# Local attention: rotary products and squares taken from PSUM, halves swapped by a negative step, and mask and minimum of two heads in two instructions

## The chip, the cores and the metric

The kernel runs on one core of one Trainium2 chip. The metric is the device time of one execution of the whole program, in microseconds. Three runs of the kernel before took 2280.73, 2284.91 and 2290.02 us; the median is 2284.91 us.

## The reference, cut to what matters

The program is a sequence of eight stages over four batches of 512 positions with 128 channels: four attention blocks (causal, relative with rotary shift, ALiBi, Shaw's relative positions) and, between them, four other blocks. The second stage, called F0 in the kernel, is the one that the change rewrites. It is a small transformer of two layers with local attention, 8 heads of 64, window 64:

```
q, k = l2norm(q) * qs, l2norm(k) * ksc
q, k = q*cos*scale + rotate_half(q)*sin*scale, k*cos/scale + rotate_half(k)*sin/scale
sim  = einsum(q * 8, k of this window and of the one before)
sim  = where((i < j) | (i > j + 64) | (j == -1), -max, sim)
out  = softmax(sim) @ v
x = x + out @ wo;  h = layernorm(shift(x));  x = x + (a * gelu(g)) @ w2
```

Here rotate_half(x) is the pair (-x2, x1) of the two halves of a head's 64 values. The causal and the ALiBi stage (class Causal and its subclass Alibi), and the rotary stage (class Rel), subtract each row's maximum before the exponential; they compute these maxima with one instruction that adds a mask to a block of scores, writes the sum to a scratch tile that nobody reads, and gives the maximum along the row.

## The kernel before, in words

All stages share the five engines (in the profile PE is TensorE, with PEld for its weight loads, DVE VectorE, ACT ScalarE, POOL GpSimd, and SP the queue that issues most transfers). Python generators, one for each strand of work (projections of the next batch, scores of this one, the block behind the attention), are stepped in turn, and a tile framework with priorities then sets the final order of the instructions of each engine. Each engine works its instructions off in that order; waits between engines, and between instructions of one engine that reuse a buffer, are semaphores. A tile of a pool with a tag and bufs=n has n buffers in turn: the instruction that writes buffer n+1 waits until the users of buffer 1 are done.

F0 treats 8 units u (4 batches, 2 layers). For each unit, qkv (from L1525) transposes the input (L208), makes for every 128 rows c three products of three matmuls each (q, k, v; L298 to L300) in a PSUM bank "b" (three banks, which the block behind the attention uses too). For q and k, ScalarE copies the bank to SBUF (L1563: the tile ta for q, kr for k), squares it (L1566, tile sq, one buffer), VectorE multiplies the two halves of each head, swapped, by a table of sines into the tile tb (L1570, two instructions of 256 elements), then the tile itself by the cosines (L1572), and sums the squares of each head (L1573). For k, GpSimd adds the two products (L1586); for q, TensorE adds them when it transposes them into a bank "t". The reciprocal norms rn come from a chain of small VectorE instructions (L327 to L336, L1589, L1591), and k is scaled by them (L1597).

scores (from L1607) computes the scores of two heads in 16 matmuls (L1620) into two banks "s". score (from L1624), called for each head, runs four times, for blocks of 128 by 128: one VectorE instruction that adds the band mask, writes the sum to sm (one buffer) and gives the row's minimum times rn into nb (L1633; the page shows it as CUSTOM_DVE_ANT_0, followed by DVE_READ_ACCUMULATOR2_ANT, which stores the minimum), and one exponential on ScalarE with nb as bias and -1 as scale (L1635; its row sum is stored by ACTIVATION_READ_ACCUMULATOR) into p (four buffers of 512). Two heads later, turn transposes p (L208), ScalarE copies it to PT (L1645), and values multiplies by v (L1664). post (from L1674) is the block behind: division (L1697), output projection (L1703), the shifted tile h whose first row is cleared by GpSimd (L1707), yb = X + b2 on GpSimd (L1712), layernorm, the gated network (L1737, L1740, L1747, L1754) and the sum (L1757, L1760).

In the other attention stages the scratch tile of the maxima is called junk: L644 (Causal and Alibi, 256 instructions each, 128 to 512 elements) and L922 (Rel, 256 of 640 elements). It has two buffers. Stage A3 has a scratch tile of the same kind, jk (L1303), with one buffer; its scores sit in L1279 to L1285.

Of the kernel before, what the change touches and what calls it, by code (L numbers as in the profile page):

```python
# [16 lines left out]
P = 128  # L17
# [565 lines left out]
class Causal(Attn):  # L583
# [49 lines left out]
    def maxima(self, t, gs):  # L633
        k, nc, pool = self.k, self.nc, self.wk
        Ks = self.Ks[t % self.nb]
        mx = pool.tile([P, 4, 4], F32, tag="mx", name=f"mx{t}", bufs=2)
        for i in range(4):
            for qc in range(4):
                n = P * (qc + 1)
                nm = max(n, 256)  # L640
                s = k.bank("s")
                nc.tensor.matmul(s[:, :nm], self.qof(0, t, i)[:, qc * P:(qc + 1) * P], Ks[:, i, :nm], start=True, stop=True)  # L642
                junk = pool.tile([P, 512], BF16, tag="junk", name=f"junk{t}{i}{qc}", bufs=2)
                nc.vector.tensor_tensor_reduce(junk[:, :n], s[:, :n], k.mask[:, 512 - n:512], 1.0, NEG,  # L644
                                               ALU.add, ALU.max, mx[:, qc, i:i + 1])
                if i == 3 and qc == 3:
                    gs.append(self.rows_out(t, mx))
                yield
# [117 lines left out]
class Rel(Attn):  # L766
# [139 lines left out]
    def maxima(self, t, gs):  # L906
# [4 lines left out]
        for i in range(4):  # L911
            for qc in range(4):
# [8 lines left out]
                junk = pool.tile([P, 640], BF16, tag="junk", name=f"junk{t}{i}{qc}", bufs=2)  # L921
# [496 lines left out]
def f0_constants():  # L1418
# [17 lines left out]
    band = np.stack([band, band], 1)  # L1436
# [4 lines left out]
class F0:  # L1441
# [3 lines left out]
    wait_rn, wait_h, wait_h7, wait_ta, na, nbt, nta, la, np, ns, npt, pk = 6, 2, 8, 2, 4, 4, 2, 2, 4, 1, 3, 0  # L1445
    banks = dict(s=2, t=2, o=1, b=3)
# [5 lines left out]
    def setup(self):  # L1452
        k, nc, d, pool = self.k, self.k.nc, self.k.d, self.early
        self.band = k.load(pool, d["c_band"], [P, 2, P], "band", BF16, eng=nc.gpsimd)
        yield from self.weights_qkv(0)
        yield from self.weights_post(0)
# [68 lines left out]
    def qkv(self, u, X, tag="t"):  # L1525
# [25 lines left out]
        for c in range(4):  # L1551
            cs = slice(c * P, (c + 1) * P)
            for s in range(3):
# [4 lines left out]
                if s == 2:  # L1558
                    nc.scalar.copy(v[:, c, :], ps)
                    yield  # L1560
                    continue
                x = kr[:, c, :] if s else pool.tile([P, 512], F32, tag="ta", name=f"ta{u}{c}", bufs=self.nta)
                nc.scalar.copy(x, ps)  # L1563
                yield
                sq = pool.tile([P, 512], F32, tag="sq", name=f"sq{u}{c}{s}", bufs=1)
                nc.scalar.activation(sq, x, AF.Square)  # L1566
                tb = pool.tile([P, 8, 64], F32, tag="tb", name=f"tb{u}{c}{s}", bufs=2)
                x3 = x.rearrange("p (h d) -> p h d", d=64)
                for a, b2 in ((0, 32), (32, 0)):
                    nc.vector.tensor_tensor(tb[:, :, a:a + 32], x3[:, :, b2:b2 + 32],  # L1570
                                            w["tab"][:, 2 * s + 1, c, None, a:a + 32].to_broadcast([P, 8, 32]), ALU.mult)
                nc.vector.tensor_tensor(x3, x3, w["tab"][:, 2 * s, c, None, :].to_broadcast([P, 8, 64]), ALU.mult)  # L1572
# [17 lines left out]
        rn = pool.tile([P, 2, 4, 8], F32, tag="rn", name=f"rn{u}", bufs=2)  # L1590
        nc.vector.tensor_copy(rn.rearrange("p s c h -> p (s c h)"), k.rsqrt(pool, sf, 64, 1))  # L1591
# [15 lines left out]
    def scores(self, u, pr):  # L1607


        k, nc = self.k, self.nc  # L1610
        qT, kT = self.S[u][:2]
        if pr == 0:
            self.den[u] = self.early.tile([P, 4, 8], F32, tag="den", name=f"den{u}", bufs=2)
        self.s = [k.bank("s") for _ in range(2)]
        with k.front():
            for w in range(8):
                c, o = w // 2, 64 * (w % 2)
                for e in range(2):
                    r = slice(64 * e, 64 * e + 64)
                    m = nc.tensor.matmul(self.s[e][o:o + 64, c * P:c * P + P], qT[r, pr, 64 * w:64 * w + 64], kT[r, pr, 64 * w:64 * w + P], start=True, stop=True)  # L1620
                    if w == e == 0 and self.emptied:
                        k.waits(m.ins, self.emptied)

    def score(self, u, h):  # L1624

        k, nc, pool = self.k, self.nc, self.pool
        rn, den, s = self.S[u][3], self.den[u], self.s[h % 2]
        p = self.p[8 * u + h] = pool.tile([P, 4, P], F32, tag="p", name=f"p{u}{h}", bufs=self.np)
        nb = pool.tile([P, 4], F32, tag="nb", name=f"nb{u}{h}", bufs=3)
        sm = pool.tile([P, 4, P], F32, tag="sm", name=f"sm{u}{h}", bufs=self.ns)  # L1630
        for c in range(4):

            m = nc.vector.tensor_tensor_reduce(sm[:, c, :], s[:, c * P:c * P + P], self.band[:, min(c, 1), :],  # L1633
                                           rn[:, 0, c, h:h + 1], 3.0e38, ALU.add, ALU.min, nb[:, c:c + 1])
            nc.scalar.activation(p[:, c, :], sm[:, c, :], AF.Exp, bias=nb[:, c:c + 1], scale=-1.0, accum_out=den[:, c, h:h + 1])  # L1635
        self.emptied = m.ins

    def turn(self, u, h):
        k, nc, pool = self.k, self.nc, self.pool
        p = self.p.pop(8 * u + h)  # L1640
# [33 lines left out]
    def post(self, u, X):  # L1674
# [32 lines left out]
        nc.gpsimd.memset(h[0:1, 0, 64:], 0.0)  # L1707
# [3 lines left out]
        yb = k.sh.tile([P, 4, P], F32, tag="r", name=f"yb{u}", bufs=1)  # L1711
        nc.gpsimd.tensor_tensor(yb, Y, w["b2"][:, None, :].to_broadcast([P, 4, P]), ALU.add)  # L1712
# [15 lines left out]
        nc.vector.tensor_tensor(xl, t, xh.bitcast(F32), ALU.subtract)  # L1728
        yield
# [51 lines left out]
    def run(self, Xs):  # L1781
# [9 lines left out]
        self.p, self.emptied = {}, None  # L1791
# [533 lines left out]
```

## Time and profile before

| | us |
|---|---|
| median of three runs | 2284.91 |
| the profiled execution | 2285.95 |
| its span | 2284.3 |
| TensorE busy (matmuls) | 2025.2 (89%) |
| VectorE busy | 1682.8 (74%) |
| ScalarE busy | 1334.6 (58%) |
| GpSimd busy | 581.1 (25%) |
| mean granted TensorE clock | 0.958 of full |

Busy time is the time in which an engine has at least one instruction running; instructions of one engine overlap a little, so that the distance from start to start of two that follow each other is shorter than their duration. By the first and last starts of their lines, the maxima of Causal (L644) run from 27.6 to 231.7 us, F0's scores from 249.0 to 654.2 us, Rel's maxima from 681.5 to 1063.3 us, and Alibi's from 1173.7 to 1425.6 us; neighbouring stages overlap at their ends, and the projections of F0's first unit run from 157.9 us on.

### The profile page before, as it was taken

To read this page: it belongs to the slowest core of one execution; us is meant where nothing else is said; L and a number is where in the kernel's file an instruction comes from. 1 tells how busy PE (TensorE), PEld (TensorE's weight loads), DVE (VectorE), ACT (ScalarE), POOL (GpSimd) and SP (SyncE) were. 2 spreads that over 40 slices of the span, in tenths; PEclk is the share of its full clock that TensorE was granted. 3 is DMA by queue.
4 is the path that set the end of the run, shared out by engine and by line. 5 is a ranking of instruction groups with operands and counts; after the bars stand their busy time and mean duration, and the time that the engine had idled before them with its cause. 6 is when DMAs were issued, how large, how long until landed. Compare 5 with 4: busy or idle time off the path is not lost.

```text
span 2284.3 us, 42095 instructions
## 1 busy us (share of the span) xinstructions
PE 2025.2 (89%) x13888; PEld 1467.8 (64%) x13888; DVE 1682.8 (74%) x5589; ACT 1334.6 (58%) x2982; POOL 581.1 (25%) x775
## 2 busy tenths in 40 slices
PE   6989787888778889898999999899899999999897
PEld 4665566666656556665788666677666666665676
DVE  5778688688878777775677877552778878778787
ACT  3656786677753456566332666332777777777632
POOL 2222212111212655555200222522111111111221
PEclk9999998899997989999999999999899999999999
DMA  6221311111341543521220330412889888788400
GB/s 185 91 75 34 98 50 44 24 28 30 109 132 33 177 144 95 154 79 34 69 65 1 116 105 30 153 68 57 202 212 213 207 195 191 187 215 202 117 5 15
DMA packets 265507, 242.31 MB, mean 106 GB/s; under 512 B 106368, under 2 KB 190634, under 8 KB 264522
## 3 DMA queue, kind: packets, MB, share of 16 engines
q1 hardware_dynamic: 260058, 222.12, 36.1%
q0 software_dynamic: 5232, 17.50, 3.3%
q8 instruction: 111, 1.82, 0.3%
q14 instruction: 106, 0.87, 0.1%
HBM read 103.03 MB, written 74.32 MB: 78 GB/s over the span
## 4 chain that ended last, share of the span: by engine, by line
PE 48%; DVE 12%; ACT 8%; POOL 5%; DMA 5%; issue 4%; SPq 1%; ACTq 0%; POOLq 0%; DVEq 0%
PE t L208 4%; PE s L2047 4%; PE o L1328 3%; PE o L967 3%; PE o L1946 3%; PE b L298 2%; PE s L298 2%; PE s L300 2%; PE s L299 2%; POOL Pt L1012 2%; PE o L691 2%; PE s L1279 2%; PE s L1280 2%; PE b L299 2%; PE b L300 1%
## 5 line engine op out<-in xcount | busy, mean ns | idle before, releaser
L922 DVE CUSTOM_DVE_ANT_0 junk<-w,a1mask 128x640 bf16<-128x640 f32 x256 | 204.4, 818 | 77.5 <-PE w L920 75.8
L208 PE MATMUL t<-ident,p 128*128 128x128 f32 x1280 | 203.5, 280 | 19.6 <-ACT p L1285 13.8
L718 ACT ACTIVATE Pt<-t 128x384 f32<-128x384 f32 (+1 forms) x384 | 178.2, 536 | 52.6 <-PE t L675 41.0
L208 PEld LDWEIGHTS t<-ident,p 128*128 128x128 f32 x1280 | 151.7, 142 | 80.0 <-ACT p L1285 35.7
L1298 ACT COPY PT<-t 128x512 f32<-128x512 f32 x256 | 150.2, 596 | 77.7 <-PE t L208 76.8
L993 ACT ACTIVATE Pt<-t 128x512 f32<-128x512 f32 x256 | 150.0, 599 | 71.9 <-PE t L992 49.1
L1285 ACT ACTIVATE p<-s,nb 128x512 f32<-128x512 f32 x256 | 178.8, 703 | 13.9 <-DVE nb L1284 7.6
L1284 DVE TENSOR_REDUCE nb<-s 128x1 f32<-128x512 f32 x256 | 175.0, 687 | 2.5
L644 DVE CUSTOM_DVE_ANT_0 junk<-s,a0mask 128x128 bf16<-128x128 f32 (+3 forms) x256 | 114.3, 486 | 41.5 <-PE s L642 40.9
L1303 DVE CUSTOM_DVE_ANT_0 jk<-p,a3right 128x496 bf16<-128x496 f32 (+3 forms) x256 | 124.1, 485 | 26.0 <-ACT p L1285 14.6
L644 DVE CUSTOM_DVE_ANT_0 junk<-s,a2mask 128x128 bf16<-128x128 f32 (+3 forms) x256 | 115.7, 485 | 28.2 <-PE s L642 27.4
L727 POOL TENSOR_SCALAR_AFFINE_SELECT Pt<-Pt 128x512 f32<-128x512 f32 x112 | 71.8, 653 | 228.7 <-ACT Pt L718 211.9
L1282 DVE TENSOR_TENSOR s<-s,W 128x160 f32<-128x160 f32 (+1 forms) x256 | 81.3, 319 | 65.5 <-PE s L1280 64.3
L1279 PE MATMUL s<-a3KT,a3QT 128*128 128x512 f32 x256 | 119.0, 467 | 7.7 <-DMA a3KT<-H 2.4
L1635 ACT ACTIVATE p<-sm,nb 128x128 f32<-128x128 f32 x256 | 101.3, 399 | 30.5 <-DVE nb L1633 29.9
L1328 PE MATMUL o<-PT,V 128*64 128x512 f32 x512 | 116.9, 599 | 0.5 <-ACT PT L1298 0.5
L1280 PE MATMUL s<-a3K,a3Q 128*128 128x512 f32 x256 | 102.7, 402 | 0.0
L1633 DVE CUSTOM_DVE_ANT_0 sm<-s,band,rn 128x128 f32<-128x128 f32 x256 | 78.4, 345 | 30.3 <-PE s L1620 22.4
L990 PE MATMUL t<-a1Q,a1K 128*128 128x512 f32 (+3 forms) x256 | 93.0, 370 | 6.1 <-ACT Pt L993 1.9
L967 PE MATMUL o<-Pt,a1va 128*32 128x128 f32 (+3 forms) x896 | 69.5, 453 | 26.9 <-POOL Pt L1012 26.8
L1933 ACT ACTIVATE sl<-s 128x512 f32<-128x512 f32 x64 | 38.1, 600 | 90.4 <-PE s L300 75.9
L1321 POOL CAST a<-at 128x256 fp32r<-128x256 f32 x32 | 13.0, 406 | 304.8 <-DMA at<-a3dpw 162.1
(497 smaller groups left out, 5983.9 us busy)
## 6 DMA issues: line engine op xcount, KB each, us to landing
W<-a3dsk SPq DMA_DIRECT2D x32, 640.0 KB
a1Q<-a1iq SPq DMA_DIRECT2D x32, 512.0 KB
a3dpw<-p SPq DMA_DIRECT2D x64, 160.0 KB
a3dpw<-p SPq DMA_DIRECT2D x64, 144.0 KB
a1K<-a1ik SPq DMA_DIRECT2D x64, 128.0 KB
a3Q<-a3dim SPq DMA_DIRECT2D x32, 256.0 KB
a3QT<-H SPq DMA_DIRECT2D x64, 128.0 KB
a3QT<-L SPq DMA_DIRECT2D x64, 128.0 KB
```

What stands on the lines that cost most here:

```text
L208: self.nc.tensor.matmul(out.bitcast(x.dtype), x, i[:n, :n], is_transpose=True, start=start, stop=stop)
L644: nc.vector.tensor_tensor_reduce(junk[:, :n], s[:, :n], k.mask[:, 512 - n:512], 1.0, NEG, ALU.add, ALU.max, mx[:, qc, i:i + 1])
L718: ready = nc.scalar.activation(Pt[:, i, z:], s[:, z:], AF.Exp, scale=sc).ins
L922: nc.vector.tensor_tensor_reduce(junk, s.rearrange("p a n -> p (a n)")[:, T - n:T + m], k.mask[:, T - n:T + m], 1.0, NEG, ALU.add, ALU.max ...
L967: m = nc.tensor.matmul(o[0][32 * i:32 * i + 32, x:y], k.vhead(va, kc, 4 * g + i), Pt[:, i, a:a + y - x], start=(kc == 0), stop=(kc == 3 an ...
L993: nc.scalar.activation(Pt[:, i, :T], s, AF.Exp, scale=sc)
L1279: nc.tensor.matmul(s, QT[:, e, qs], KT[:, e, :], start=True, stop=False)
L1280: nc.tensor.matmul(s, Q2[:, e, qs], K2[:, e, :], start=False, stop=True)
L1284: nc.vector.tensor_reduce(nb, s, AX.X, ALU.min)
L1285: nc.scalar.activation(p[:, e, :], s, AF.Exp, bias=nb, scale=-1.0, accum_out=den[:, qc, 2 * un + e:2 * un + e + 1])
L1298: self.copied[t] = nc.scalar.copy(PT[e][:, :, qc * P:qc * P + P], tb.rearrange("p (c n) -> p c n", n=P)).ins
L1328: m = nc.tensor.matmul(o[64 * e:64 * e + 64, :], V[:, kc, h * 64:h * 64 + 64], PT[e][:, kc, :], start=(kc == 0), stop=False)
```

## The change

- The copy L1563 goes. The square reads the PSUM bank, and so do the two products with the tables. The two instructions that swapped the halves become one of 512 elements: its input runs over the two halves with a negative step.
- The scores of two heads go to one tile of two banks (one buffer, as many banks as before). One VectorE instruction adds the mask to all 1024 columns and writes to p, one takes the eight minima of each row, and one of 8 columns multiplies them by rn. The exponentials work in place in p, with nb as bias, and take minus rn as scale, a column for each block, from a third part of rn. p has two buffers of 1024 in place of four of 512, sm is gone. The explicit wait of the scores on the last mask instruction goes too: the framework's own wait on the tile remains.
- The mask has four copies of its block, in place of two.
- The clearing of a row of h goes from GpSimd to VectorE; yb is computed later, behind the split of the transposed h.
- junk, in Causal, Alibi and Rel, has one buffer in place of two.

```diff
--- before.py
+++ after.py
@@ -640,7 +640,7 @@
                 nm = max(n, 256)
                 s = k.bank("s")
                 nc.tensor.matmul(s[:, :nm], self.qof(0, t, i)[:, qc * P:(qc + 1) * P], Ks[:, i, :nm], start=True, stop=True)
-                junk = pool.tile([P, 512], BF16, tag="junk", name=f"junk{t}{i}{qc}", bufs=2)
+                junk = pool.tile([P, 512], BF16, tag="junk", name=f"junk{t}{i}{qc}", bufs=1)
                 nc.vector.tensor_tensor_reduce(junk[:, :n], s[:, :n], k.mask[:, 512 - n:512], 1.0, NEG,
                                                ALU.add, ALU.max, mx[:, qc, i:i + 1])
                 if i == 3 and qc == 3:
@@ -918,7 +918,7 @@
                 else:
                     nc.tensor.matmul(s[:, 0, T - n:], self.qof(0, t, i)[:, qs], Ks[:, i, 0:n], start=True, stop=True)
                 nc.tensor.matmul(s[:, 1, :m], self.qof(1, t, i)[:, qs], Ks[:, i, T - m:T], start=True, stop=True)
-                junk = pool.tile([P, 640], BF16, tag="junk", name=f"junk{t}{i}{qc}", bufs=2)
+                junk = pool.tile([P, 640], BF16, tag="junk", name=f"junk{t}{i}{qc}", bufs=1)
                 nc.vector.tensor_tensor_reduce(junk, s.rearrange("p a n -> p (a n)")[:, T - n:T + m], k.mask[:, T - n:T + m], 1.0, NEG,
                                                ALU.add, ALU.max, mx[:, qc, i:i + 1])
                 if i == 3 and qc == 3:
@@ -1433,7 +1433,7 @@
     i = np.arange(P)[:, None] % 64
     j = np.arange(P)[None, :]
     band = np.where((i <= j) & (j <= i + 64), 0.0, 1.0e20).astype(np.float32)
-    band = np.stack([band, band], 1)
+    band = np.stack([band] * 4, 1)
     band[:64, 0, :64] = 1.0e20
     return {"c_rot": np.ascontiguousarray(rot), "c_band": band, "c_sel8": heads(8)}
 
@@ -1442,8 +1442,8 @@
 
 
     nm, span, keep = "f0", "first", True
-    wait_rn, wait_h, wait_h7, wait_ta, na, nbt, nta, la, np, ns, npt, pk = 6, 2, 8, 2, 4, 4, 2, 2, 4, 1, 3, 0
-    banks = dict(s=2, t=2, o=1, b=3)
+    wait_rn, wait_h, wait_h7, wait_ta, na, nbt, nta, la, np, npt, pk = 6, 2, 8, 2, 4, 4, 2, 2, 2, 3, 0
+    banks = dict(s=1, t=2, o=1, b=3)
 
     def __init__(self, k):
         self.k, self.nc = k, k.nc
@@ -1451,7 +1451,7 @@
 
     def setup(self):
         k, nc, d, pool = self.k, self.k.nc, self.k.d, self.early
-        self.band = k.load(pool, d["c_band"], [P, 2, P], "band", BF16, eng=nc.gpsimd)
+        self.band = k.load(pool, d["c_band"], [P, 4, P], "band", BF16, eng=nc.gpsimd)
         yield from self.weights_qkv(0)
         yield from self.weights_post(0)
 
@@ -1559,17 +1559,16 @@
                     nc.scalar.copy(v[:, c, :], ps)
                     yield
                     continue
+
                 x = kr[:, c, :] if s else pool.tile([P, 512], F32, tag="ta", name=f"ta{u}{c}", bufs=self.nta)
-                nc.scalar.copy(x, ps)
+                x3, p3 = (y.rearrange("p (h d) -> p h d", d=64) for y in (x, ps))
+                sq = pool.tile([P, 512], F32, tag="sq", name=f"sq{u}{c}{s}", bufs=1)
+                nc.scalar.activation(sq, ps, AF.Square)
+                tb = pool.tile([P, 8, 64], F32, tag="tb", name=f"tb{u}{c}{s}", bufs=2)
+                nc.vector.tensor_tensor(tb.rearrange("p h (a d) -> p h a d", a=2), ps.rearrange("p (h a d) -> p h a d", a=2, d=32)[:, :, ::-1],
+                                        w["tab"][:, 2 * s + 1, c].rearrange("p (a d) -> p a d", a=2)[:, None].to_broadcast([P, 8, 2, 32]), ALU.mult)
+                nc.vector.tensor_tensor(x3, p3, w["tab"][:, 2 * s, c, None, :].to_broadcast([P, 8, 64]), ALU.mult)
                 yield
-                sq = pool.tile([P, 512], F32, tag="sq", name=f"sq{u}{c}{s}", bufs=1)
-                nc.scalar.activation(sq, x, AF.Square)
-                tb = pool.tile([P, 8, 64], F32, tag="tb", name=f"tb{u}{c}{s}", bufs=2)
-                x3 = x.rearrange("p (h d) -> p h d", d=64)
-                for a, b2 in ((0, 32), (32, 0)):
-                    nc.vector.tensor_tensor(tb[:, :, a:a + 32], x3[:, :, b2:b2 + 32],
-                                            w["tab"][:, 2 * s + 1, c, None, a:a + 32].to_broadcast([P, 8, 32]), ALU.mult)
-                nc.vector.tensor_tensor(x3, x3, w["tab"][:, 2 * s, c, None, :].to_broadcast([P, 8, 64]), ALU.mult)
                 nc.vector.tensor_reduce(ss[:, s, c, :], sq.rearrange("p (h d) -> p h d", d=64), AX.X, ALU.add)
                 yield
                 for _ in range(self.wait_ta if u == 0 else 0):
@@ -1587,8 +1586,10 @@
 
         sf = ss.rearrange("p s c h -> p (s c h)")
         nc.vector.tensor_scalar(sf, sf, 1e-24, None, ALU.max)
-        rn = pool.tile([P, 2, 4, 8], F32, tag="rn", name=f"rn{u}", bufs=2)
-        nc.vector.tensor_copy(rn.rearrange("p s c h -> p (s c h)"), k.rsqrt(pool, sf, 64, 1))
+        rn = pool.tile([P, 3, 4, 8], F32, tag="rn", name=f"rn{u}", bufs=2)
+        y = k.rsqrt(pool, sf, 64, 1)
+        nc.vector.tensor_copy(rn[:, 0:2].rearrange("p s c h -> p (s c h)"), y)
+        nc.vector.tensor_scalar(rn[:, 2].rearrange("p c h -> p (c h)"), y[:, 0:32], -1.0, None, ALU.mult)
         for _ in range(self.wait_rn):
             yield
         for c in range(5):
@@ -1607,37 +1608,36 @@
     def scores(self, u, pr):
 
 
-        k, nc = self.k, self.nc
-        qT, kT = self.S[u][:2]
+
+        k, nc, pool = self.k, self.nc, self.pool
+        qT, kT, _, rn = self.S[u]
         if pr == 0:
             self.den[u] = self.early.tile([P, 4, 8], F32, tag="den", name=f"den{u}", bufs=2)
-        self.s = [k.bank("s") for _ in range(2)]
+        s = k.wide("s")
         with k.front():
             for w in range(8):
                 c, o = w // 2, 64 * (w % 2)
                 for e in range(2):
                     r = slice(64 * e, 64 * e + 64)
-                    m = nc.tensor.matmul(self.s[e][o:o + 64, c * P:c * P + P], qT[r, pr, 64 * w:64 * w + 64], kT[r, pr, 64 * w:64 * w + P], start=True, stop=True)
-                    if w == e == 0 and self.emptied:
-                        k.waits(m.ins, self.emptied)
+                    nc.tensor.matmul(s[o:o + 64, e, c * P:c * P + P], qT[r, pr, 64 * w:64 * w + 64], kT[r, pr, 64 * w:64 * w + P], start=True, stop=True)
+        sm = self.p[4 * u + pr] = pool.tile([P, 2, 4, P], F32, tag="p", name=f"p{u}{pr}", bufs=self.np)
+        nb = pool.tile([P, 2, 2, 4], F32, tag="nb", name=f"nb{u}{pr}", bufs=2)
+        nc.vector.tensor_tensor(sm, s.rearrange("p e (c n) -> p e c n", n=P), self.band[:, None].to_broadcast([P, 2, 4, P]), ALU.add)
+
+        nc.vector.tensor_reduce(nb[:, 0], sm, AX.X, ALU.min)
+        nc.vector.tensor_tensor(nb[:, 1], nb[:, 0], rn[:, 0, :, 2 * pr:2 * pr + 2].rearrange("p c e -> p e c"), ALU.mult)
+        self.nb = nb[:, 1]
 
     def score(self, u, h):
 
-        k, nc, pool = self.k, self.nc, self.pool
-        rn, den, s = self.S[u][3], self.den[u], self.s[h % 2]
-        p = self.p[8 * u + h] = pool.tile([P, 4, P], F32, tag="p", name=f"p{u}{h}", bufs=self.np)
-        nb = pool.tile([P, 4], F32, tag="nb", name=f"nb{u}{h}", bufs=3)
-        sm = pool.tile([P, 4, P], F32, tag="sm", name=f"sm{u}{h}", bufs=self.ns)
-        for c in range(4):
-
-            m = nc.vector.tensor_tensor_reduce(sm[:, c, :], s[:, c * P:c * P + P], self.band[:, min(c, 1), :],
-                                           rn[:, 0, c, h:h + 1], 3.0e38, ALU.add, ALU.min, nb[:, c:c + 1])
-            nc.scalar.activation(p[:, c, :], sm[:, c, :], AF.Exp, bias=nb[:, c:c + 1], scale=-1.0, accum_out=den[:, c, h:h + 1])
-        self.emptied = m.ins
+        rn, den, e = self.S[u][3], self.den[u], h % 2
+        p = self.p[4 * u + h // 2][:, e]
+        for c in range(4):
+            self.nc.scalar.activation(p[:, c, :], p[:, c, :], AF.Exp, bias=self.nb[:, e, c:c + 1], scale=rn[:, 2, c, h:h + 1], accum_out=den[:, c, h:h + 1])
 
     def turn(self, u, h):
         k, nc, pool = self.k, self.nc, self.pool
-        p = self.p.pop(8 * u + h)
+        p = self.p[4 * u + h // 2][:, h % 2]
         t = k.bank("t")
         for c in range(4):
             k.tr(t[:, c * P:c * P + P], p[:, c, :])
@@ -1704,12 +1704,10 @@
         Y = X
         nc.vector.tensor_tensor(Y, Y, y.rearrange("p (c n) -> p c n", c=4), ALU.add)
         h = k.sh.tile([P, 4, P], F32, tag="os", name=f"h{u}", bufs=1)
-        nc.gpsimd.memset(h[0:1, 0, 64:], 0.0)
+        nc.vector.memset(h[0:1, 0, 64:], 0.0)
         nc.sync.dma_start(h[:, :, 0:64], Y[:, :, 0:64])
         k.up(h[:, :, 64:], Y[:, :, 64:])
         nc.sync.dma_start(h[0:1, 1:4, 64:], Y[P - 1:P, 0:3, 64:])
-        yb = k.sh.tile([P, 4, P], F32, tag="r", name=f"yb{u}", bufs=1)
-        nc.gpsimd.tensor_tensor(yb, Y, w["b2"][:, None, :].to_broadcast([P, 4, P]), ALU.add)
         if l:
             x0 = k.load(k.sh, self.x0[b], [P, 4, P], f"x0{b}", tag="os")
         yield
@@ -1726,6 +1724,8 @@
         xl = k.sh.tile([P, T], F32R, tag="ot", name=f"hfl{u}", bufs=2)
         nc.scalar.copy(xh, t)
         nc.vector.tensor_tensor(xl, t, xh.bitcast(F32), ALU.subtract)
+        yb = k.sh.tile([P, 4, P], F32, tag="r", name=f"yb{u}", bufs=1)
+        nc.gpsimd.tensor_tensor(yb, Y, w["b2"][:, None, :].to_broadcast([P, 4, P]), ALU.add)
         yield
         g = self.early.tile([P, 3, T], F32, tag="g", name=f"g{u}", bufs=1)
         for i in range(3):
@@ -1788,7 +1788,7 @@
         nc.gpsimd.dma_start(self.sel, k.d["c_sel8"])
         self.v2 = pool.tile([P, 4, 512], F32, name="f0v2")
         nc.gpsimd.memset(self.v2[0:64, 0:1], 0.0)
-        self.p, self.emptied = {}, None
+        self.p = {}
         self.item = 0
         gs, A, B = [], [self.operands_of(Xs)], [self.posts(Xs)]
         la = self.la
```

## The prediction

> **What bounds the kernel now.** The profiled execution took 2285.95 us (span 2284.3), 1.0 above the median of the three runs; I sum against it and take 1 us off at the end. First the page's busy shares, then the busy time of the four stages that the diff touches, a stretch for each: Causal, F0, Rel, Alibi.
>
> ```profile
> PE 2025.2 (89%) x13888; PEld 1467.8 (64%) x13888; DVE 1682.8 (74%) x5589; ACT 1334.6 (58%) x2982; POOL 581.1 (25%) x775
> ...
> 20.00:232.00 212.00, 188.84 (x1247) 125.89 (x1248) 163.19 (x678) 119.21 (x249) 53.98 (x74) 0.98 0.27 81
> 249.00:660.00 411.00, 335.43 (x3518) 260.33 (x3517) 337.72 (x1198) 302.16 (x867) 77.58 (x92) 0.93 0.22 58
> 681.00:1065.00 384.00, 331.65 (x2251) 237.80 (x2250) 292.03 (x820) 211.76 (x382) 200.59 (x251) 0.92 0.35 107
> 1174.00:1428.00 254.00, 244.80 (x1708) 180.58 (x1706) 197.27 (x826) 132.74 (x264) 45.24 (x61) 0.99 0.20 59
> ```
>
> Columns: stretch, length, then busy us of PE, weight load, DVE, ACT, POOL. In F0 no engine is full: PE 335 and DVE 338 of 411, ACT 302. The stage is set by a chain that changes engine all the time. In Causal PE is busy 89% and DVE 77%, in Alibi 96% and 78%, in Rel 86% and 76%: there PE leads and DVE follows closely.
>
> Next the chain that ended last, asked for in stretches from 385 to 660 us (it is not traced further back in F0). I added its pieces by line. In 275 us it holds 26.0 us of exponentials with their accumulator reads (L1635, 131 pieces, so some 66 exponentials), 8.35 us of the copies L1563 (16), 11.3 us of L1570 (25 instructions), 9.6 us of the mask instruction L1633. A part of it, start and length first:
>
> ```profile
> 429.76 1.10 PE s L1620 x32
> ...
> 430.96 0.35 DVE sm L1633
> 431.31 0.02 DVE nb L1633
> ...
> 431.35 0.89 ACT p L1635 x4
> 432.24 0.47 ACT qT L1584
> 432.71 0.49 ACT kr L1563
> ...
> 433.30 0.76 DVE tb L1570 x2
> ```
>
> The reader sees both chains that the change cuts into: scores, first mask instruction, exponentials; and copy, then products. For the whole stage I scale by 411/275 = 1.49.
>
> Last, how the scratch instructions stand on DVE (timeline: start and length in us). Two of L644 with two buffers, and two of A3's jk, which has one:
>
> ```profile
> 182.48 0.69 DVE L644 CUSTOM_DVE_ANT_0 junk<-s,a0mask 128x512 bf16<-128x512 f32 x1
> 183.09 0.08 DVE L644 DVE_READ_ACCUMULATOR2_ANT mx<- 128x1 f32 x1
> 183.09 0.28 DVE L644 CUSTOM_DVE_ANT_0 junk<-s,a0mask 128x128 bf16<-128x128 f32 x1
> ...
> 1620.72 0.27 DVE L1303 CUSTOM_DVE_ANT_0 jk<-p,a3right 128x112 bf16<-128x112 f32 x1
> 1620.91 0.09 DVE L1303 DVE_READ_ACCUMULATOR2_ANT at<- 128x1 f32 x1
> 1621.15 0.28 DVE L1303 CUSTOM_DVE_ANT_0 jk<-p,a3right 128x112 bf16<-128x112 f32 x1
> ```
>
> With two buffers the next one starts together with the accumulator read of the one before; with one buffer it starts 0.144 us after that read's end. The read takes 0.08, so the start moves by 0.224 us.
>
> **The change part by part.**
>
> *One buffer for junk.* In the order of the built kernel 179 of Causal's 256, 128 of Rel's and 151 of Alibi's stand directly behind another one, and each waits for the accumulator read just before it. In the trace of before 154, 82 and 127 such pairs ran without a gap. 363 x 0.224 = 81 us more on DVE: that is the upper end, nothing the lower, since TensorE leads and DVE often waits for it (before L644 40.9 us in Causal, before L922 75.8 us). What counts is where DVE has no idle time. I went through the three stages in stretches of 10 us, added 0.224 us for each gapless pair, and took what exceeds the 10 us. In Causal, 30 to 40 us:
>
> ```profile
> 30.00:40.00 10.00, 9.54 (x31) 6.18 (x32) 9.15 (x45) 1.87 (x4) 1.56 (x3) 1.00 0.34 98
> 40.00:50.00 10.00, 9.24 (x56) 6.24 (x59) 9.46 (x38) 6.98 (x15) 2.50 (x4) 1.00 0.61 166
> ```
>
> 9.15 + 17 x 0.224 = 13.0, 3.0 too much; then 9.46 + 11 x 0.224 = 11.9, 1.9 too much. All in all 6.8 us in Causal, 0.6 in Rel, 3.7 in Alibi: 11 us. With stretches of 5 us it is 10.2, 3.7 and 5.8, 20 us; three banks "s" and two "w" let the engines drift apart by some microseconds, so I take **+11**. Behind a waiting junk stand the layernorms, the splits and the divisions on DVE, and TensorE waits for the bank. The Trainium skill, "VectorE: DVE Perf Modes", section "The DRAIN you can't avoid", holds against this: it measured that a semaphore after each of eight copies costs nothing over one at the end. The pair of jk above says otherwise, so the trace decides; by the page this term would be 0 and the sum 11 us less.
>
> *The copies go.* L1563 stands on the chain with 8.35 us; TensorE's bank is then read by DVE directly. 8.35 x 1.49 = **-12.5**. On ACT the 64 copies free 64 x 0.48 (start to start) = 31 us, most of it beside other work.
>
> *Two products in one.* L1570 is 0.34 us from start to start, one of 512 elements 0.60 (L1572). On the chain 25 of the first become 12.5 of the second, 11.3 - 7.5 = 3.8, x 1.49 = **-5.7**. Some of it are instructions stretched to 1.1 us and more beside L1586 on GpSimd. No row shows a negative step: 0.60 each, or twice that at worst, which would be 64 x 0.60 = 38 us on DVE; I take 0.60, as all 512-element forms here cost 0.60, from PSUM (L1697) or SBUF (L1597).
>
> *The exponentials.* The scale becomes a column. A row with a scale column against one without, same shape and both from PSUM: L2027 0.690 and L1933 0.599 us, 0.091 more. L1635 has one column already (its bias); none here has two, so the bounds are 0 and 0.104 (L1285, 0.703, over L993, 0.599); I take 0.091. 256 x 0.091 = 23 us on ACT; on the chain 66 x 0.091 x 1.49 = **+9**. The Trainium skill, "ScalarE: Activation LUTs", section "What ACT_TABLE_LOAD costs", says that each such column adds about 93 ns; by it the estimate is 9 us as well, and a second column would not be free.
>
> *Mask and minimum in two.* Eight L1633 take 0.27 us each from start to start with their reads, 32 x 8 x 0.27 = 70 us. Now 32 x (1.12 + 1.12 + 0.2) = 78 us: an instruction of 1024 elements is an estimate of 0.60 + 2 x 0.26 by the step between the rows of 256 (0.34) and 512 (0.60). That is 8 us more on DVE, beside what the products give back, **+1** on the chain. But the first exponential now waits for 2.5 us plus waits on DVE itself, against 0.37 us. In the 275 us the chain enters the exponentials 9 times through one first mask instruction straight behind the scores: 9 x 2.2 x 1.49 = 30 us if nothing covers it, 0 if the next pair's scores are always ahead. They can be: the add frees both banks after 1.12 us, and sm no longer waits for ACT (6.8 us). I take a third, **+10**.
>
> *The bank "b" is held longer*: till the square and two products are done, some 0.7 us more than a copy. TensorE waits for L1563 7.9 + 4.2 us, 16 times; 16 x 0.7 = 11 us at most, 0 if another of three banks is free. In DVE's queue the products may stand behind an add that waits for transposes of p two pairs back. I take **+3**.
>
> *Clearing h, and yb.* GpSimd waits 30.8 us in L1707, but nobody waits for L1707, and yb is needed some 20 us later: 0. On DVE the clearing stands behind the split of h, when the transposes that read h are done: 8 x 0.14 us. The larger mask is loaded once, under Causal: 0. TensorE's matmuls and SP's queue keep their count.
>
> The sum: 11 - 12.5 - 5.7 + 9 + 1 + 10 + 3 = +15.8. 2285.95 + 15.8 = 2302, and 2301 against the median.
>
> **The rivals.** What a measurement of this kernel can tell from no change is about 0.5%, 11 us: 2273.5 to 2296.3.
>
> *F0 gains and the junk hides* (faster). Mechanism: TensorE sends each pair's scores early, so the 10 for the first exponential and the 3 for the bank are 0, and the waits of ACT for nb (29.9 us) shrink by a third, -10; junk costs 4, DVE's idle time in front of L644 taking the rest. 4 - 12.5 - 5.7 + 9 + 1 - 10 = -14: 2271. With the second column free it is 2262. For it: 41 and 76 us of DVE idle time before the junk lines. Against it: the stretches with no idle time left. It decides from the point where TensorE runs the scores at least 2.5 us ahead of the exponentials.
>
> *Latency of the pair* (slower still). The first exponential pays in full, +30, the bank +11, junk 20: 20 - 18.2 + 9 + 1 + 30 + 11 = +53, or 2338; half-way from the forecast 2320. For it: ACT already waits 35 times for nb.
>
> *The buffer changes nothing*: no back-to-back pair is held, junk 0, the rest as forecast: +5, 2290, no change.
>
> **How the numbers follow.** Forecast 0.40 (2290 to 2312), faster rival 0.25, latency 0.23, no effect of the buffer 0.12. The forecast's lower quarter lies under 2296, so no change has 0.12 + 0.10 and a little of the faster rival, 0.25; faster 0.23; slower 0.52. The range from 2264 to 2330 takes in the two gain cases and the latency case up to its middle.
>
> **What would show it.** After: pairs of L644 and L922 with a gap behind the accumulator read, and more PE waits for mx in Causal; exponentials at 0.49 us; no L1563; DVE in F0 about as busy as before, ACT some 10 us less; ACT's wait for nb above 30 us. I am wrong if the stages with junk keep their length, or if F0 alone shrinks by over 15 us.

## The result, and the profile after

Measured side by side, the changed kernel takes 2350.3 us (median of 4 runs, 2348.5 to 2356.8) and the kernel before 2285.0 us: a ratio of 1.0283, 95% interval 1.0258 to 1.0307. It is slower by 65 us, where the forecast was 16 slower, outside the stated range of 2264 to 2330. The profiled execution has a span of 2348.0 us.

First the page's busy shares of the changed kernel, then its four stages in stretches drawn around their new lengths (stretch, length, then busy us of PE, weight load, DVE, ACT, POOL):

```profile
PE 2058.5 (88%) x13888; PEld 1472.2 (63%) x13888; DVE 1704.7 (73%) x5125; ACT 1320.0 (56%) x2918; POOL 575.8 (25%) x767
```

```profile
20.00:242.00 222.00, 197.28 (x1250) 125.67 (x1250) 171.56 (x671) 115.14 (x242) 52.16 (x74) 1.00 0.26 79
249.00:690.00 441.00, 350.12 (x3505) 265.92 (x3502) 333.94 (x741) 297.07 (x812) 77.71 (x87) 0.91 0.21 54
715.00:1107.00 392.00, 336.61 (x2249) 237.16 (x2248) 298.61 (x820) 209.97 (x382) 200.01 (x251) 0.92 0.35 106
1215.00:1492.00 277.00, 259.34 (x1713) 183.79 (x1715) 207.01 (x825) 132.16 (x264) 46.60 (x63) 0.97 0.19 55
```

F0 is longer, and no engine in it is fuller: 334 of 441 us on DVE. DVE and ACT have less to do in it than before; PE's matmuls, no more in number, are busy 15 us longer, at a granted clock (the figure behind POOL's) of 0.91 in place of 0.93. The rest of the growth is waits. By first and last starts, the time came in four places:

| us | before | after | more |
|---|---|---|---|
| to F0's first scores (Causal before it) | 249.0 | 258.3 | 9.3 |
| F0's first scores to Rel's first maxima | 432.5 | 457.0 | 24.5 |
| Rel's maxima, first to last | 381.8 | 390.7 | 8.9 |
| Alibi's maxima, first to last | 252.1 | 276.1 | 24.0 |

The four sum to 66.7 us; the span grew by 63.7, so the other stages took 3 us less. (Alibi's maxima, L644, start from 1174.2 to 1426.3 us before; the 1173.7 to 1425.6 us given for them above are those of the scores L642, as are Causal's.) Rel and Alibi hold nothing of the change but the one buffer for junk; Causal also has the projections of F0's first unit beside it. How its instructions now stand on DVE (timeline, start and length), in Causal:

```profile
185.38 0.08 DVE L644 DVE_READ_ACCUMULATOR2_ANT mx<- 128x1 f32 x1
185.60 0.69 DVE L644 CUSTOM_DVE_ANT_0 junk<-s,a0mask 128x512 bf16<-128x512 f32 x1
186.22 0.08 DVE L644 DVE_READ_ACCUMULATOR2_ANT mx<- 128x1 f32 x1
```

The next one starts 0.14 us behind the end of the read, no longer together with it. In F0, the waits (engine, line, what it waited for: us in total, times, longest):

```profile
DVE tb L1568 <- ACT sq L1566: 27.2, 29, 3.4
...
DVE p L1625 <- PE s L1622: 21.7, 8, 12.6
...
ACT sq L1566 <- DVE ss L1572: 19.0, 13, 4.0
...
DVE p L1625 <- PE t L208: 15.3, 10, 2.7
...
ACT p L1636 <- DVE nb L1628: 14.9, 14, 3.0
```

The first is new: the product with the sines waits for the Square of the same bank. The third has grown; the Square, whose tile sq has one buffer, waits for the sum over the previous one, and before it did so for 7.9 us:

```profile
ACT sq L1566 <- DVE ss L1573: 7.9, 10, 1.8
```

And the groups of instructions of the change (busy us, mean ns, idle time before them):

```profile
L1636 ACT ACTIVATE p<-p,nb,rn 128x128 f32<-128x128 f32 x253 | 122.1, 486 | 15.1 <-DVE nb L1628 14.9
...
L1625 DVE TENSOR_TENSOR p<-s,band 128x1024 f32<-128x1024 f32 x32 | 39.0, 1219 | 37.0 <-PE s L1622 21.7 <-PE t L208 15.3
L1627 DVE TENSOR_REDUCE nb<-p 128x8 f32<-128x1024 f32 x32 | 38.7, 1210 | 0.3
L1568 DVE TENSOR_TENSOR tb<-b,tab 128x512 f32<-128x512 f32 x56 | 38.4, 686 | 29.4 <-ACT sq L1566 27.2 <-issue 2.2
```

### The profile page after: what moved, and what is told of

Same layout as the page of the kernel before. It is cut to its first block, busy times and chain, and to the rows that moved or that the text cites. A ratio compares the mean times of both kernels' runs of the same rounds, so it can differ in the third digit from the quotient of the medians.

```text
span 2348.0 us, 41653 instructions
## 1 busy us (share of the span) xinstructions
PE 2058.5 (88%) x13888; PEld 1472.2 (63%) x13888; DVE 1704.7 (73%) x5125; ACT 1320.0 (56%) x2918; POOL 575.8 (25%) x767
## 4 chain that ended last, share of the span: by engine, by line
PE 51%; DVE 19%; ACT 8%; POOL 6%; DMA 4%; issue 4%; SPq 1%; ACTq 0%; DVEq 0%; POOLq 0%
PE t L208 5%; PE s L2047 4%; PE o L1328 4%; PE o L967 3%; PE o L1946 2%; PE b L298 2%; DVE junk L922 2%; PE o L691 2%; PE t L675 2%; PE s L642 2%; POOL Pt L1012 2%; PE s L298 2%; PE b L299 2%; ACT p L1636 2%; PE b L300 2%
## 5 line engine op out<-in xcount | busy, mean ns | idle before, releaser
L922 DVE CUSTOM_DVE_ANT_0 junk<-w,a1mask 128x640 bf16<-128x640 f32 x256 | 209.7, 819 | 77.8 <-PE w L920 61.6
L644 DVE CUSTOM_DVE_ANT_0 junk<-s,a0mask 128x128 bf16<-128x128 f32 (+3 forms) x256 | 124.5, 486 | 44.3 <-PE s L642 21.2
L644 DVE CUSTOM_DVE_ANT_0 junk<-s,a2mask 128x128 bf16<-128x128 f32 (+3 forms) x256 | 124.7, 487 | 38.5 <-PE s L642 17.4
L1636 ACT ACTIVATE p<-p,nb,rn 128x128 f32<-128x128 f32 x256 | 123.6, 486 | 15.1 <-DVE nb L1628 14.9
L642 PE MATMUL s<-a0K,a0Q 128*128 128x256 f32 (+2 forms) x256 | 90.6, 398 | 13.0 <-DVE mx L644 6.8
L642 PE MATMUL s<-a2K,a2Q 128*128 128x256 f32 (+2 forms) x256 | 89.1, 388 | 11.3 <-DVE mx L644 10.8
L1585 POOL TENSOR_TENSOR kr<-kr,tb 128x512 f32<-128x512 f32 x32 | 41.0, 1280 | 229.2 <-DVE kr L1570 202.8
```

The costliest lines, as they stand in the source:

```text
L922: nc.vector.tensor_tensor_reduce(junk, s.rearrange("p a n -> p (a n)")[:, T - n:T + m], k.mask[:, T - n:T + m], 1.0, NEG, ALU.add, ALU.max ...
L1636: self.nc.scalar.activation(p[:, c, :], p[:, c, :], AF.Exp, bias=self.nb[:, e, c:c + 1], scale=rn[:, 2, c, h:h + 1], accum_out=den[:, c, h ...
```

## The experiments

All times are medians; "cost" is the ratio to the kernel before, less 1, times 2285 us. The kernel before took 2288.0 us beside e1 to e4, 2285.0 beside e5 to e12 and 2286.2 beside e13 to e15.

| run | us | ratio, 95% interval | cost, us |
|---|---|---|---|
| e1: before, junk with one buffer | 2325.3 | 1.0158 (1.0138 to 1.0178) | +36 |
| e2: after, junk with two | 2323.6 | 1.0143 (1.0114 to 1.0173) | +33 |
| e3: before, rotary edit alone | 2278.3 | 0.9961 (0.9942 to 0.9979) | -9 |
| e4: e2 without the rotary edit | 2306.4 | 1.0077 (1.0057 to 1.0097) | +18 |
| e5: before, scale from a column | 2284.5 | 0.9999 (0.9987 to 1.0011) | 0 |
| e6: e4, add, minimum, product per head | 2301.2 | 1.0069 (1.0046 to 1.0091) | +16 |
| e7: e6, each head's scores in their own bank | 2300.5 | 1.0075 (1.0053 to 1.0096) | +17 |
| e8: e2, Square behind the products | 2280.6 | 0.9981 (0.9967 to 0.9996) | -4 |
| e9: e3, Square behind the products | 2263.6 | 0.9912 (0.9891 to 0.9934) | -20 |
| e10: before, clearing and yb moved | 2286.1 | 1.0014 (1.0002 to 1.0027) | +3 |
| e11: e4, clearing and yb as before | 2308.2 | 1.0110 (1.0087 to 1.0133) | +25 |
| e12: e8, clearing and yb as before | 2281.6 | 0.9983 (0.9966 to 0.9999) | -4 |
| e13: e11, old mask instruction, in place | 2284.5 | 0.9994 (0.9984 to 1.0004) | -1 |
| e14: e11, masked sum in a tile of its own | 2315.3 | 1.0128 (1.0113 to 1.0143) | +29 |
| e15: after, Square behind the products | 2320.0 | 1.0149 (1.0132 to 1.0166) | +34 |

**e1 and e2: the one buffer, alone and taken back.** To make room for the second buffer, e2 loads the larger mask only when F0 starts; so do the kernels built on it (e4, e6, e7, e8, e11 to e14).

```diff
-                junk = pool.tile([P, 512], BF16, tag="junk", name=f"junk{t}{i}{qc}", bufs=2)
+                junk = pool.tile([P, 512], BF16, tag="junk", name=f"junk{t}{i}{qc}", bufs=1)
```

> The kernel before with one buffer for junk in Causal, Rel and Alibi, nothing else. Theory A: of the 65 us that the change costs, the three stages with junk carry the 43 by which their first and last starts moved apart (Causal 9, Rel 9, Alibi 24), all of it from the wait of each junk on the accumulator read before it: 2285 + 43 = 2328. Theory B: those stages grew because the order of the engines' instructions changed or because F0 handed them a worse start; the buffer alone costs what the prediction said, 11 us or less: 2296 or below.

> The changed kernel with two buffers for junk again; so that it fits into SBUF, the mask of four blocks is loaded at the start of F0 and not under Causal. Theory A: 2350 - 43 = 2307, Alibi's maxima take 252 us again, as before, in place of 276. Theory B: 2340 or more.

e1 alone costs 36 us, as theory A has it. In the profiled execution Causal is 8.6 us longer, Rel 9.4, Alibi 24.3, F0 0; that is 42, as this execution was the slowest of four and its span is 43 us above that of before. In e2, Rel (382.7) and Alibi (252.3) are back at the lengths of before, and the changed kernel is 32 us faster than with one buffer. The 43 that theory A expected to get back did not all come: e2 took 2323.6 us in place of 2307. Its first scores of F0 still start 4 us late (253.3 us), and from there to Rel's first maxima it took 459.4 us, against 457.0 in the change. Where the larger mask is loaded differs in e2 too and was not tried by itself; e1, which leaves the mask alone, shows the cost of the buffer without it. Who waited for L644, before and in e1 (us, times):

```profile
  PEld s L642: 20.6, 52
...
  PE s L642: 5.2, 11
```

```profile
  PEld s L642: 56.0, 115
  PE s L642: 17.9, 30
```

TensorE's waits for the maxima of Causal and Alibi went from 25.8 to 73.9 us. DVE's 0.22 us per pair arrive, in good part, at the engine that leads.

**e3 and e4: the two rewrites of F0, each without the other.** e3 makes the rotary part of the diff in the kernel before; e4 takes it out of e2.

> The kernel before with the rotary edit alone: no copy, square and two products from the bank, halves by a negative step. Theory C: the first product waits for the square of the same bank (in the profile of after it never starts less than 0.03 us behind the square's end), and the square waits for the sum of the squares before (one sq buffer), so the copy's place on the chain is taken by the square and a loop of square, two products and sum appears: 10 to 20 us slower, 2295 to 2305. Theory D: the edit gives what the prediction summed, 12.5 + 5.7 us, and the loss in F0 is all in the scores: 2267 to 2275.

> The changed kernel without the rotary edit and with two buffers for junk (mask loaded at F0's start): mask and minimum of two heads, exponentials with a column as scale, the moved clearing and yb remain. Theory C: they cost 2 to 12 us, 2287 to 2297. Theory D: they cost more than the 24 us by which F0 grew, as the rotary edit gave 18 back: 2320 or more.

Alone, the rotary edit gains 9 us; mask and minimum with the rest cost 18. Their sum is +9, but e2, which has both, costs 33. Some 24 us, known to about 9 from the intervals, come only from the two together. Both times lie between the ranges of theory C and theory D, so neither theory was right as it stood.

**e8 and e9: the Square behind the products.** One line moves; nothing is computed differently.

```diff
-                nc.scalar.activation(sq, ps, AF.Square)
                 tb = pool.tile([P, 8, 64], F32, tag="tb", name=f"tb{u}{c}{s}", bufs=2)
...
                 nc.vector.tensor_tensor(x3, p3, w["tab"][:, 2 * s, c, None, :].to_broadcast([P, 8, 64]), ALU.mult)
+                nc.scalar.activation(sq, ps, AF.Square)
```

> The changed kernel with two buffers for junk (mask loaded at F0's start) and the square issued behind the two products. Theory C (the loop of square, products and sum makes the rotary edit cost in company what it gives alone): VectorE's waits for the square in front of the first product (25.6 us) go, 8 to 17 us are given back, 2306 to 2315. Rival: the bank is held by the same three readers in any order, and TensorE waits as before: 2320 to 2327.

> The kernel before with the rotary edit alone, and the square issued behind the two products. Theory C (it is the square ahead of the products that costs, by the loop of sum, square, product): at least the 5 us that the prediction's 18 less the 10 of the rotary edit alone leave open, 2262 to 2272. Rival (the square ahead costs only where the pair's mask and minimum stand in VectorE's queue too): as the rotary edit alone, 2273 to 2280.

In company it gives back 37 us (e2 to e8), more than twice what theory C put as the most, and alone 11 (e3 to e9), as theory C has it. The gain lies in F0: from its first scores to Rel's first maxima it takes 459.4 us in e2 and 428.3 in e8, 425.8 in e3 and 411.4 in e9. In the changed kernel none of the 64 products with the sines starts before the end of the Square on the same bank, and in 61 of them the trace shows DVE waiting on a semaphore that this Square sets. In e9 the wait lies on the other side (waits of F0):

```profile
ACT sq L1569 <- DVE ta L1568: 9.1, 11, 2.7
ACT sq L1569 <- DVE kr L1568: 9.0, 8, 1.7
...
DVE ss L1571 <- ACT sq L1569: 4.7, 8, 1.1
```

Now ACT waits for DVE, 18 us in all, and the sum waits 5; the products no longer wait for the Square. e9 is the fastest kernel of the study: 2263.6 us, some 20 less than before and 85 less than the change. It beats both.

**e5: the column as scale.**

```diff
-            nc.scalar.activation(p[:, c, :], sm[:, c, :], AF.Exp, bias=nb[:, c:c + 1], scale=-1.0, accum_out=den[:, c, h:h + 1])
+            nc.scalar.activation(p[:, c, :], sm[:, c, :], AF.Exp, bias=nb[:, c:c + 1], scale=self.mone, accum_out=den[:, c, h:h + 1])
```

> The kernel before with one change: the 256 local exponentials take their scale of -1 from a column of SBUF. Theory E: each is 0.09 us longer (0.49 in place of 0.40), 23 us on ScalarE, of which the prediction put 9 on the chain: 2285 to 2300, median 2296 beside 2287. Theory F: ScalarE has room in F0 (302 of 411 us busy), the column is hidden: within 3 us of before.

The exponential's group before, and in e5:

```profile
L1635 ACT ACTIVATE p<-sm,nb 128x128 f32<-128x128 f32 x256 | 101.3, 399 | 30.5 <-DVE nb L1633 29.9
```

```profile
L1635 ACT ACTIVATE p<-sm,nb,f0mone 128x128 f32<-128x128 f32 x256 | 124.4, 489 | 22.7 <-DVE nb L1633 22.2
```

Each grows by 90 ns, close to the 93 ns of the Trainium skill ("ScalarE: Activation LUTs", "What ACT_TABLE_LOAD costs"), 23 us in all, and the kernel is not slower. A third of it came out of ACT's waits for nb (29.9 us before, 22.2 here); where ACT, busy 302 of 411 us in F0 before, absorbed the rest no view names.

**e6 and e7: the pair taken apart.** e6 splits the wide instructions by head; e7 also gives each head's scores a bank of their own.

```diff
-        nc.vector.tensor_tensor(sm, s.rearrange("p e (c n) -> p e c n", n=P), self.band[:, None].to_broadcast([P, 2, 4, P]), ALU.add)
-        nc.vector.tensor_reduce(nb[:, 0], sm, AX.X, ALU.min)
...
+        for e in range(2):
+            nc.vector.tensor_tensor(sm[:, e], s[:, e].rearrange("p (c n) -> p c n", n=P), self.band, ALU.add)
+            nc.vector.tensor_reduce(nb[:, 0, e], sm[:, e], AX.X, ALU.min)
```

> The run without the rotary edit, with the mask and the minimum taken for each head (two instructions of 512 columns for each, the tile of two banks unchanged), so that the first exponential of a pair waits for about 1.4 us of VectorE in place of 2.6, and the banks come free as late as before or later. Theory G (latency of the first exponential): 5 to 12 us are given back, 2295 to 2301. Theory H (the next pair's scores wait for the add, as both banks are one tile with one buffer): nothing given back, 2304 to 2312.

> As the run before, but each head's scores in a bank of its own, two buffers as in the kernel before, so that a bank comes free behind the add of its own head. Theory H: TensorE's waits for the add in front of the scores (13.7 us in the run without the rotary edit) fall below 5, and 8 to 15 us are given back: 2291 to 2298. Theory G alone: the same time as the run before.

Neither gives back more than the intervals. TensorE's waits for the add fell only from 13.7 to 8.5 us in e7, so this is no full test of the shared tile of two banks; e13 below, which shares it too and is as fast as before, shows that it is not the cause. Nor is the clock: F0's stretch had a granted clock of 0.90 in e6 and 0.92 in e7, and took 447.5 and 448.5 us. Halving the instructions might be thought to clear the wait of the first exponential, but does not: see e13.

**e10 to e12: the clearing and yb.** Moved alone (e10), put back without the rotary edit (e11), put back beside the Square behind the products (e12).

> The kernel before with the clearing of h on VectorE and yb computed later, nothing else. Theory I (these two, which the prediction put at nothing, make the 18 us of the run without the rotary edit, by waits of TensorE for h and by the late yb): 2292 to 2303. Theory K (they are hidden, as predicted): 2281 to 2289.

> The run without the rotary edit, with the clearing on GpSimd and yb early again: only mask and minimum of two heads and the exponentials' column are left. Theory I: 2283 to 2291. Theory K: the mask and the minimum of two heads make the 18 us, 2298 to 2308.

> The changed kernel with two buffers for junk, the square behind the products, and the clearing on GpSimd and yb early. Theory I: 2262 to 2272, faster than both. Theory K: as the run with the square behind, 2276 to 2285.

The move costs 0.5 to 6 us alone by its interval, nothing in e12, and putting it back does not speed up e4. What e11 holds beyond the kernel before, mask and minimum of two heads with the column, costs 25 us.

**e13 and e14: the form or the buffers?** Both start from e11. e13 keeps p as it is in the change (1024 wide, two buffers, exponentials in place) but masks block by block with the old instruction; e14 keeps the two wide instructions but gives the masked sum a tile of its own, and p three buffers of 512.

```diff
-        nc.vector.tensor_tensor(sm, s.rearrange("p e (c n) -> p e c n", n=P), self.band[:, None].to_broadcast([P, 2, 4, P]), ALU.add)
-        nc.vector.tensor_reduce(nb[:, 0], sm, AX.X, ALU.min)
...
+        for e in range(2):
+            for c in range(4):
+                nc.vector.tensor_tensor_reduce(sm[:, e, c], s[:, e, c * P:c * P + P], self.band[:, c], rn[:, 0, c, 2 * pr + e:2 * pr + e + 1], 3.0e38, ALU.add, ALU.min, self.nb[:, e, c:c + 1])
```

> The kernel with only mask and minimum of two heads and the column left took 2308 us (1.011). Here its two wide instructions are replaced by the old one-instruction mask-and-minimum of each block of 128 columns, which writes straight into the wide tile of the pair; the exponentials go in place over it, and that tile has two buffers, as in the changed kernel. The bias is the minimum itself and the scale the constant -1. If the two-buffer tile in place is the cause (the mask of a pair waits until the transposes of the pair two before have read it), the time stays at 2298 to 2310 us. If the two-instruction form is (nothing of a pair can be exponentiated before both instructions have passed over all eight blocks), it falls back to 2281 to 2290 us.

> The two wide instructions stay, but the masked sum goes into a tile of its own (one buffer of 1024 columns) and the exponentials write from it into tiles of 512 columns with three buffers, so that the add no longer waits for transposes of an earlier pair, but for the exponentials of the pair before. If the place in the buffers is the cause, 2283 to 2293 us against 2308; if the two-instruction form is, 2298 to 2312 us.

e13 is as fast as before, e14 no faster than e11: the two-instruction form, with the column that goes with it, costs the time, and the place in the buffers does not. (In e14 the add waits for the exponentials of the pair before instead of the transposes, so it exchanges one wait for another; e13, with the buffers of the change, is the stronger of the two.) The loss lies in F0: first scores to Rel's first maxima take 432.5 us before, 429.5 in e13, 450.5 in e11 and 460.1 in e14. DVE's work does not explain it: in these stretches DVE is busy 354 us in e13 and 359 in e11. The timeline of e11 around one pair (start, length):

```profile
300.82 1.23 DVE L1626 TENSOR_TENSOR p<-s,band 128x1024 f32<-128x1024 f32 x1 [2.65 <-PE s L1623]
...
301.96 0.41 DVE L1570 TENSOR_TENSOR tb<-ta,tab 128x256 f32<-128x256 f32 x1
302.29 1.21 DVE L1628 TENSOR_REDUCE nb<-p 128x8 f32<-128x1024 f32 x1
...
303.42 0.41 DVE L1570 TENSOR_TENSOR tb<-ta,tab 128x256 f32<-128x256 f32 x1
303.75 0.17 DVE L1629 TENSOR_TENSOR nb<-nb,rn 128x8 f32<-128x8 f32 x1
...
303.96 0.49 ACT L1637 ACTIVATE p<-p,nb,rn 128x128 f32<-128x128 f32 x1 [1.01 <-DVE nb L1629]
```

and of e13:

```profile
296.74 0.35 DVE L1628 CUSTOM_DVE_ANT_0 p<-s,band,rn 128x128 f32<-128x128 f32 x1 [4.31 <-PE s L1623]
297.01 0.08 DVE L1628 DVE_READ_ACCUMULATOR2_ANT nb<- 128x1 f32 x1
297.01 0.35 DVE L1628 CUSTOM_DVE_ANT_0 p<-s,band,rn 128x128 f32<-128x128 f32 x1
297.19 0.41 ACT L1635 ACTIVATE p<-p,nb 128x128 f32<-128x128 f32 x1 [1.02 <-DVE nb L1628]
```

In e13 ACT follows DVE by one block, 0.45 us; in e11 it starts 3.1 us behind the add, with two other instructions of DVE's queue between the three. From the starts in the traces, over all 32 pairs: first exponential behind the first mask instruction, mean 0.6 us before, 1.2 in e13, 5.2 in e11, and still 4.3 in e6, which fits with how little e6 changed. In e11 it takes 4.5 us on the mean from the start of the add to the end of the product, and 2.3 of these are other instructions of DVE. At the end of a unit nothing is left to cover that. From the start of a unit's last scores to the end of its last exponential (mean of 8 units) it takes 10.0 us before, 12.9 in e13, 21.9 in e11, 21.1 in e6 and 19.5 in e14. The first three pairs' scores go out earlier in e11 (the last pair's follow the first's by 26.9 us in place of 34.7), which returns a part, and a unit comes every 55.9 us in place of 53.7 (52.9 in e13). The block behind the attention, and through it the next layer, starts that much later. e11 and e13 differ in the column too; e5 showed it free beside the old instruction, and beside the new ones it was not tried by itself. At 0.09 us for each of a pair's eight exponentials it would add, by estimate, 0.7 us to the end of a unit, of the 9 us between e13 and e11.

**e15: do the two losses add up?** The change as it stands, with only the Square moved as in e8.

> The change as it stands, one buffer for the leftovers included, with the Square alone issued behind the two products. If the costs add up, the 2281 us of the kernel with two buffers and the Square behind, and 37 to 42 us for the one buffer: 2316 to 2324 us. If the one buffer costs much less once the Square is out of the way, it ends below 2305 us.

They do: one buffer costs 38 us between e8 and e15, 32 between e2 and the change, 36 alone.

## Why the prediction was wrong

Slower was right. The sum was +16; the runs put it together as -20 (rotary edit with the Square behind, e9) + 16 (mask and minimum with the column beside it, e9 to e8) + 37 (the Square in front, e8 to e2) + 32 (junk, e2 to the change) = +65. These are steps along one path from kernel to kernel, so they must close on 65; each is known to some 5 to 9 us from the intervals. The forecast's terms for the same steps were -18, +20, at most +3, and +11: two steps failed, the Square, which had no term of its own, and junk, which was put at a third of what it cost. The rival "latency of the pair" (2338) came nearest, and it too had junk at 20 and no term for the Square. Neither of the two signs by which I would have been wrong appeared; the forecast fell by the size of its terms.

- *One buffer for junk, +11.* The mechanism was right, to the 0.224 us and the waits for mx; the size was off by three, inside the bounds of 0 to 81. The step that failed counted only what exceeded a stretch of 10 us of DVE time, as if the score banks let a delay be made up within 10 us. Of 34 us that 151 pairs add in Alibi, where TensorE was 96% busy, 24 arrived (3.7 forecast); of 40 in Causal 9 (6.8 forecast), of 29 in Rel 9 (0.6). TensorE's waits for the maxima of Causal and Alibi grew by 48 us in e1, so the delay was not made up. What the Trainium skill measured on eight copies, that a semaphore after each costs nothing ("VectorE: DVE Perf Modes", "The DRAIN you can't avoid"), does not carry over to these instructions with an accumulator read: here the wait cost 36 us (e1).
- *The copies go, -12.5, and two products in one, -5.7.* With the Square behind the products the rotary edit gains 20 us against 18.2 forecast, which may be luck, as the pricing was weak (below). In the order of the diff it gained 9, and beside the pair form it lost 15 (e4 to e2). The failed step took the copy out of the chain and put nothing in its place. The chain of before already showed 7.0 us of Squares in those 275 us; as first reader of the bank the Square took the copy's place, with one buffer sq that ties it to the sum one block back. "TensorE's bank is then read by DVE directly" left out that DVE's read waits for the Square (27.2 us in the change).
- *The exponentials, +9.* The duration was right (90 ns), the price was 0: I multiplied a longer instruction by its share of the chain, and e5 shows that a longer piece on the chain need not lengthen the stage.
- *Mask and minimum, +1 and +10.* The mechanism, a first exponential that waits for everything, is what e13 supports; the size was 25 us without the rotary edit and 16 beside e9's, both with the column, against 11 (20 with the column). I priced one wait of 2.2 us per pair; the traces show 4.6 us more (5.2 for 0.6), as 2.3 us of DVE's other work stand between the instructions, and the loss falls at the unit's end. The estimate of 1.12 us for an instruction of 1024 elements was good: from start to start they take 1.14 and 1.13 us.
- *Bank "b" held longer, +3; clearing and yb, 0.* The first can't be told from the Square's place. The second was 3 alone and 0 in company.
- *What no term held:* the Square in front costs 11 us alone and 37 beside the pair form. Why it costs so much more in company stays open. One reading is that the sum, which frees sq, stands behind add and minimum of 2.4 us on DVE; that was not isolated, and DVE's waits for the Square differ by less (15.4 us in e3, 25.6 in e2).

Pricing by the chain's lines was itself weak: traced over 249 to 690 us, the chain holds 47 us of exponentials in e13 and 24 in e9, though both run the same 256, of 401 and 397 ns.

Of the signs named, the gap behind the read, the waits for mx, exponentials of 0.49 us, a DVE about as busy in F0 and a less busy ACT came (15 us less over the whole program, 5 in F0's stretch). The wait of ACT for nb did not: 14.9 us in place of more than 30. The latency shows at the end of the units instead.

## What to carry to other kernels

When two engines are to read one PSUM bank, decide which goes first: the one that feeds the chain, and the side result behind it. One instruction over many blocks in place of a stream of small ones can cost hardly more engine time and still lose, since its consumer can't follow block by block; look at the end of a unit, where nothing covers the latency. A second buffer for a scratch tile that nobody reads can be worth its memory where its instructions stand back to back and the leading engine waits for them: in Alibi it was worth 24 us for 151 such pairs, in Rel 9 for 128.

## What was not expected of the hardware

- A scratch tile's single buffer cost 32 to 38 us here over 512 + 256 instructions, though the wait is on an instruction of the same engine that stands directly ahead.
- The halves swapped by a negative step cost next to nothing: 686 ns for 512 elements from PSUM, against 678 to 680 for the product without it (L1570).
- An add of 1024 elements over two PSUM banks took 1219 ns and a minimum 1210: 2.27 us per pair from start to start (1.14 and 1.13), against 8 x 0.27 = 2.2 us of the block instructions.
